# A planned instruction order: activation-table loads taken out of the plan and written in afterwards

## The chip, the cores and the metric

The kernel runs on one core of a Trainium2 chip. A core has four engines that compute: PE (TensorE, matrix products), DVE (VectorE), ACT (ScalarE, which applies functions such as exp from a loaded table and also copies), and POOL (GpSimd). SP (SyncE) issues most DMAs. Each engine runs its own instructions strictly in the order in which they stand in its queue, and waits for the others at semaphores. The metric is device time of one execution in microseconds (us).

## The reference, cut to what matters

The input is 8 sequences of 256 tokens with 128 channels in float32. Eight blocks follow each other; after each one stands `x = layernorm(x + block(x))`:

1. a gated linear recurrence (sigmoid gates, exp, running product and running sum along the sequence);
2. two layers of local attention (8 heads of 64, window 64, l2-normalised queries and keys), each with a GELU feed-forward of width 341;
3. a selective scan ("mamba": silu, softplus, and 16 states for each of 256 inner channels, stepped along the sequence);
4. a mixture of 32 experts, one for each token, capacity 80;
5. two attentions with 16 heads and a feed-forward each, over chunks of 32 tokens and across chunks;
6. a mixture of 8 experts, two for each token, capacity 320, and a shared expert of width 1024;
7. causal attention with 16 heads of 8, rotated and decaying by head;
8. a linear layer with ternary weights and a bias.

## The kernel before

The kernel has six stages (`STAGES`): `rglru` (block 1 for the first four sequences), `local_mamba` (block 1 for the other four, blocks 2 and 3), `moe1` (4), `chunked` (5), `moe2` (6) and `typed` (7 and 8). In `local_mamba` eight sequences pass through attention and then the scan as a software pipeline; four sequences are alive at a time. For each sequence the scan runs eight rounds (lines 1295 to 1300): ACT makes four decay factors `da` with exp, DVE forms a product `hs`, scans it, forms a second product, and PE sums the result into `y`. A round costs about 5 us of DVE.

Mixtures are routed on the chip. For `moe1`, `route1` computes a row number for each token, in two pieces: tiles 0 to 13 (the first seven sequences), then tiles 14 and 15 (line 1512 writes the numbers `put`, line 1523 the numbers `get`). `scatter` (line 1616) then issues one indirect DMA on POOL for each tile of 128 rows, which writes them to the table `places` in memory. Plain DMAs (`got<-places`, line 1636) bring the table back once all 16 are done, and the experts' matmuls start with the transposes `bt` (line 1643). For `moe2`, `route2` does the same with 32 indirect writes; the results come back by indirect gathers (line 1651) on POOL, most of them made to wait, one each, for a silu of the shared expert.

**Who sets the order.** The program text emits all instructions. Then `_Order` takes the list and reorders it. `plan` is a list scheduler: it walks through a model of the five queues, and whenever an engine is free it takes, of the instructions that are ready, the one with the lowest `rank`. A rank is the instruction's place by priority plus a hand-tuned offset from `BIAS` (engine, tile name, stage). How long an instruction occupies its engine, and when its result is out, comes from the table `LENGTHS` (nanoseconds, two numbers). `impose` then pins each engine's queue to the planned order. The times in the plan decide nothing but order.

**ACT's tables.** exp and ln come from one table set, silu, gelu and sigmoid from three others. A function whose set isn't loaded needs a load first (`ACT_TABLE_LOAD` in the trace, `LoadActFuncSet` in the program). The kernel asks for the exp-and-ln set itself, by `exp_ln`, which emits a load at a fixed place: after the sigmoids (line 1017), after the gelus (line 1194), after the silus (line 1245), and at a few more places; `keep` ties it to ACT's instruction just before. In `moe1` a load of the silu set stands behind the last routing exp (line 1528). For all other functions the compiler puts a load right in front of an instruction whose set is not the one it finds in place. In the planner a load is an instruction of its own: `group` puts it into group 1 with exp and ln, `change` charges nothing for it, and its length is 1178 or 1283 ns; a change of group among ACT's functions is charged with `TABLE` (1283 ns) as well. `STAY` is what a change of group costs in rank: 70 for PE (where the groups are array shapes) and 310 for ACT.

Lines in the text and in the profile are those of the kernel before. In the kernel after, the same statements stand up to 17 lines away.

Of the kernel before, what the change touches and what calls it, by code (L numbers as in the profile page):

```python
# [309 lines left out]
class _Order:  # L310
# [12 lines left out]
    STAY = dict(PE=70, ACT=310)  # L323
    BIAS = {
        "ACT  1": 495, "ACT  3": -495, "ACT d 2": -1445, "ACT e 4": -700, "ACT e 6": 370, "ACT fh 4": -30, "ACT four 4": 630, "ACT four 5": -345,
        "ACT ge 2": 385, "ACT got 3": 50, "ACT got 5": 590, "ACT k 2": -275, "ACT kp 4": -40, "ACT lakq 2": -75, "ACT lavp 2": -95, "ACT lg 2": 620,
        "ACT lnrs 1": 225, "ACT lnrs 2": -280, "ACT lnsq 2": 40, "ACT ot 6": 75, "ACT ptsb 2": -740, "ACT qsq 2": -5, "ACT r 2": -70, "ACT rg 1": -590,
        "ACT rg 2": -320, "ACT rn 2": 55, "ACT rs 4": -50, "ACT rs 6": -25, "ACT s 6": -190, "ACT savp 2": -5, "ACT sg 3": 560, "ACT sh 5": -250,
        "ACT spl 1": -410, "ACT spt 1": -15, "ACT st 6": 460, "ACT v 2": 25, "ACT xc 2": -2725, "ACT xchunked 2": -400, "ACT xchunked 4": -390,
        "ACT xs 2": 10, "ACT xsq 4": -660, "DVE ab 4": 720, "DVE bt 3": -1225, "DVE bt 5": 190, "DVE centre 0": -205, "DVE d 2": -10,  # L330
        "DVE decaypart 4": -240, "DVE e 2": 50, "DVE four 5": 105, "DVE fs 4": 10, "DVE gate 2": -345, "DVE gate 5": -320, "DVE get 2": 180, "DVE get 4": 5,
        "DVE get 5": 850, "DVE got 4": -40, "DVE h 2": 5, "DVE h 5": -525, "DVE hs 2": 5, "DVE k 5": -680, "DVE lares 2": -200, "DVE lg 4": 665,
        "DVE nm 2": -135, "DVE nm 6": -95, "DVE oh 2": -285, "DVE oh 4": 2440, "DVE oh 5": -180, "DVE ptsb 2": 20, "DVE ptsb 6": -250, "DVE put 2": 190,
        "DVE put 4": 480, "DVE q 5": 470, "DVE q 6": 785, "DVE r 2": -120, "DVE rc 2": -270, "DVE rc 4": 175, "DVE route 2": -345, "DVE s 2": 20,
        "DVE s 5": -95, "DVE s 6": 1585, "DVE sares 2": 30, "DVE sel 4": -50, "DVE sg 3": -250, "DVE sm 4": 365, "DVE spt 1": 810, "DVE st 6": 150,
        "DVE sum 2": -705, "DVE t 5": 400, "DVE th 4": 650, "DVE u 2": 255, "DVE vec 2": 50, "DVE we 4": -30, "DVE wlocal 2": 1325, "DVE xc 2": -1830,
        "DVE xla 4": -580, "DVE xlf 4": 75, "DVE xlocal 2": -860, "DVE xmoe 6": 10, "DVE xpf 4": -10, "DVE xrglru 2": 205, "DVE xsa 4": 485, "DVE ys 3": 100,
        "DVE z 4": -190, "PE a 2": 50, "PE acc 5": 10, "PE b 2": 30, "PE bt 3": 1010, "PE bt 5": -580, "PE cum 2": 80, "PE cum 4": -1270, "PE fold 2": 105,
        "PE g 2": -700, "PE gate 1": -345, "PE gate 2": 345, "PE hps 4": -15, "PE kps 4": 95, "PE lg 2": 205, "PE lin 6": -1140, "PE ln 1": 355,
        "PE ln 2": -45, "PE o 6": -910, "PE out 4": -35, "PE pg 5": -20, "PE proj 5": 100, "PE proj 6": -570, "PE ps 4": -455, "PE pt 2": -25,  # L340
        "PE pt 4": -125, "PE pu 3": 2550, "PE pu 5": -720, "PE py 3": 740, "PE qkt 2": -1425, "PE raw 2": -1360, "PE rows 2": 585, "PE sc 2": -60,
        "PE sc 4": 30, "PE sc 6": -1215, "PE v 5": 470, "PE v 6": -20, "PE vps 2": 1025, "PE vps 4": -10, "PE wo 2": 60, "PE wo 6": -855, "PE wout 2": -95,
        "PE xps 2": -790, "PE y 2": 20, "PE z 2": 40, "PE zt 4": -20, "POOL biasrows 3": -595, "POOL e 4": 415, "POOL e 6": -305, "POOL got 5": 490,
        "POOL km 5": 665, "POOL mean 0": 635, "POOL one 0": 395, "POOL places 2": -70, "POOL places 5": -240, "POOL q 5": 50, "POOL q 6": -325,
        "POOL rest 4": -990, "POOL rg 1": -25, "POOL rows 4": 85, "POOL ss 2": -20, "POOL t 2": 595, "POOL u 2": 110, "POOL zero 0": -35,
        "POOL zeros 1": -385, "SP bc 2": 200, "SP cst 3": -455, "SP got 3": 535, "SP got 5": 505, "SP outdram 6": 275, "SP places 1": 1460,
        "SP rottable 0": 45, "SP routetables 0": 495, "SP rows 4": -370, "SP scales 2": 40, "SP vec 0": -1475, "SP wattn 2": 15, "SP wmoe 2": -150,
        "SP wmoe 4": -150, "SP wmoe 5": -100, "SP xs 2": -660,
# [88 lines left out]
    def group(self, i):  # L437
        x, e, op = self.ops[i]
        if e == "PE":
            up = lambda v: 32 if v <= 32 else 64 if v <= 64 else P  # L440
            ap = x.ins[1].bass_ap.ap
            return up(ap[0][1]), up(int(np.prod([k for _, k in list(ap)[1:]])))
        if e == "ACT":
            return 1 if op == "LoadActFuncSet" else self.SETS.get(str(x.func).split(".")[-1]) if op == "Activation" else None
        return None
# [319 lines left out]
class _Kernel:  # L765
# [125 lines left out]
    def exp_ln(self, last=None):  # L891

        i = self.nc.scalar.preload_act_table_set("natural_log_exp_and_others")
        if last is not None:
            self.issue_after([i], last)
# [1504 lines left out]
```

## Time and profile before

| what | value |
|---|---|
| median of 3 runs | 1695.54 us (1694.59 to 1696.02) |
| the profiled execution, its own time | 1695.66 us |
| span of that execution in the trace | 1692.0 us |
| mean granted TensorE clock | 0.947 |
| busy: PE, DVE, ACT, POOL | 1442.4, 1138.2, 976.5, 579.2 us |
| share of the chain of waits: PE, DVE, ACT, "issue", POOL, DMA | 49, 23, 11, 9, 5, 2% |
| `rglru` and the start of attention, 0 to 60 us: busy PE, DVE, ACT | 25.1, 33.7, 32.0 us |
| `local_mamba`, about 60 to 800 us | PE busy 601.2, DVE 602.5, ACT 551.2 of 740 us |
| `moe1` with its routing, about 800 to 860 us | PE busy 33.1 of 60 us |
| `chunked`, about 860 to 1285 us | PE busy 409.9 of 425 us |
| `moe2`, about 1285 to 1455 us | PE busy 156.3 of 170 us |
| `typed`, about 1455 to 1692 us | PE busy 216.8 of 237 us |

The span is the time from the first to the last instruction on the core; the execution's own time is 3.66 us more. In the views, a row of a table by stretches gives the stretch, its length, then for PE, weight loads (PEld), DVE, ACT and POOL the busy time and the number of instructions, then the granted clock, the DMA share and GB/s. A row of a timeline gives start, duration, engine, line, operation and tiles as out<-in; in brackets stands how long the engine sat idle before and what ended that.

### The profile page before, as it was taken

How to read it: one execution, taken by the hardware profiler on the slowest of the kernel's cores; microseconds unless marked ns; L12 is line 12 of the kernel's file. 1: busy time of each engine (PE TensorE's matmuls, PEld its weight loads, DVE VectorE, ACT ScalarE, POOL GpSimd, SP SyncE). 2: the span in 40 equal slices, each digit the busy share in tenths (PEclk: the TensorE clock that was granted, in tenths of full speed). 3: DMA queues.
4: the chain of work that ended last, by engine and by line, in shares of the span. 5: the costliest groups of instructions: out<-in, count | busy, mean ns of one | idle time of the engine just before them, and what ended most of it. 6: DMA issues, size and time to landing. Idle time of an engine off the chain costs nothing.

```text
span 1692.0 us, 28693 instructions
## 1 busy us (share of the span) xinstructions
PE 1442.4 (85%) x10858; PEld 932.5 (55%) x10858; DVE 1138.2 (67%) x2182; ACT 976.5 (58%) x2661; POOL 579.2 (34%) x535
## 2 busy tenths in 40 slices
PE   2688897979788877676679999999997998999997
PEld 1355553545454544343557776766674764566664
DVE  5755579898989898689354656566445332588885
ACT  3777887787877868644135554545443222366654
POOL 1344462616263423100331222221214004567573
PEclk7799999999999998899789999999997998999998
DMA  5000012121212213266310000000102121000000
GB/s 193 1 1 1 1 39 63 39 63 39 63 39 63 64 38 97 66 196 242 111 47 2 8 14 11 7 8 5 46 2 68 47 82 30 18 5 4 8 4 10
DMA packets 45113, 77.97 MB, mean 46 GB/s; under 512 B 5580, under 2 KB 21988, under 8 KB 43824
## 3 DMA queue, kind: packets, MB, share of 16 engines
q1 hardware_dynamic: 39648, 70.02, 13.8%
q0 software_dynamic: 3216, 5.07, 1.1%
q8 instruction: 85, 1.39, 0.3%
q10 hardware_dynamic: 2112, 1.05, 0.2%
q14 instruction: 52, 0.43, 0.1%
HBM read 66.87 MB, written 10.76 MB: 46 GB/s over the span
## 4 chain that ended last, share of the span: by engine, by line
PE 49%; DVE 23%; ACT 11%; issue 9%; POOL 5%; DMA 2%; another core or an unknown queue 0%; SPq 0%; ACTq 0%; DVEq 0%; POOLq 0%
PE vps L863 7%; PE kps L863 6%; PE sc L863 5%; PE out L863 4%; DVE hs L1299 3%; DVE hs L1300 3%; PE pu L863 3%; PE pg L863 3%; PE pt L974 3%; DVE hs L1297 2%; PE o L863 2%; ACT e L1146 2%; PE hps L863 2%; PE py L863 2%; PE acc L863 2%
## 5 line engine op out<-in xcount | busy, mean ns | idle before, releaser
L863 PE MATMUL y<-hs,ident 128*128 128x512 f32 x256 | 136.7, 647 | 30.2 <-DVE hs L1300 29.9
L1151 POOL TENSOR_TENSOR e<-e,rc 128x1024 f32<-128x1024 f32 x32 | 79.6, 2486 | 228.3 <-DVE rc L1150 227.6
L1299 DVE TENSOR_TENSOR_SCAN hs<-da,hs 128x1024 f32<-128x1024 f32 x64 | 154.1, 2409 | 0.1
L2250 ACT ACTIVATE e<-sc,nm 128x128 f32<-128x128 f32 (+1 forms) x256 | 105.1, 426 | 64.1 <-DVE nm L2245 55.2
L974 PE MATMUL pt<-ident,e 128*128 128x128 f32 x768 | 119.2, 281 | 18.0 <-POOL e L1151 12.4
L1295 ACT ACTIVATE da<-d,na 128x255 f32<-128x255 f32 x256 | 110.5, 508 | 22.5 <-DVE hs L1299 20.2
L1146 ACT ACTIVATE e<-sc,nm,rn 128x128 f32<-128x128 f32 x256 | 114.7, 468 | 10.9 <-DVE nm L1141 10.5
L974 PEld LDWEIGHTS pt<-ident,e 128*128 128x128 f32 x768 | 88.4, 143 | 56.3 <-issue 19.2
L2253 POOL TENSOR_TENSOR e<-e,rc 128x1024 f32<-128x1024 f32 x48 | 91.1, 1897 | 65.6 <-DVE rc L2252 65.5
L1829 POOL TENSOR_TENSOR e<-e,rc 128x512 f32<-128x512 f32 x32 | 33.9, 1059 | 226.1 <-DVE rc L1828 173.4
L1098 POOL TENSOR_TENSOR t<-t,t 128x512 f32<-128x512 f32 x64 | 84.1, 1316 | 61.1 <-DVE t L1085 56.0
L1651 POOL DMA_INDIRECT got<-ybuf,get x48 | 45.7, 952 | 169.0 <-DMA ybuf<-ys 87.6
L1804 ACT COPY kp<-kps 128x512 f32<-128x512 f32 x128 | 74.8, 585 | 48.5 <-PE kps L863 46.7
L1297 DVE TENSOR_TENSOR hs<-u,bc 128x1024 f32<-128x1024 f32 x64 | 87.5, 1384 | 6.2 <-POOL u L1284 5.5
L863 PEld LDWEIGHTS y<-hs,ident 128*128 128x128 f32 x256 | 47.5, 204 | 77.9 <-DVE hs L1300 47.5
L1300 DVE TENSOR_TENSOR hs<-hs,bc 128x1024 f32<-128x1024 f32 x64 | 87.5, 1369 | 0.0
L863 PE MATMUL qk<-w_local,h 128*128 128x512 f32 x128 | 71.1, 644 | 13.0 <-DVE t L1085 6.2
L976 DVE COPY ptsb<-pt 128x512 f32<-128x512 f32 x104 | 69.0, 677 | 17.0 <-PE pt L974 16.0
L1840 ACT COPY vs<-vps 128x512 f32<-128x512 f32 x64 | 37.4, 584 | 67.5 <-PE vps L863 56.8
L863 PE MATMUL vps<-sa_vp,x_lf 128*32 128x512 f32 x512 | 69.8, 594 | 0.0
L976 ACT COPY ptsb<-pt 128x512 f32<-128x512 f32 x88 | 51.4, 584 | 31.3 <-PE pt L974 30.7
L2245 DVE TENSOR_REDUCE nm<-sc 128x4 f32<-128x1024 f32 (+1 forms) x48 | 58.3, 1215 | 15.2 <-PE sc L863 14.6
(380 smaller groups left out, 3800.0 us busy)
## 6 DMA issues: line engine op xcount, KB each, us to landing
bc<-xs SPq DMA_DIRECT2D x128, 256.0 KB
w_moe<-in_e_dram SPq DMA_DIRECT2D x16, 768.0 KB
w_attn<-in_w_dram SPq DMA_DIRECT2D x4, 1024.0 KB
w_local<-in_w_dram SPq DMA_DIRECT2D x2, 1557.0 KB
places<-zeros SPq DMA_DIRECT2D x2, 1280.0 KB
got<-places SPq DMA_DIRECT2D x6, 256.0 KB
ybuf<-ys SPq DMA_DIRECT2D x8, 160.0 KB
x_in<-in_x_dram SPq DMA_DIRECT2D x1, 1024.0 KB
```

Source lines behind the costliest of these rows:

```text
L863: return self.nc.tensor.matmul(out, lhsT, rhs, start=start, stop=stop)
L974: self.last = self.nc.tensor.transpose(pt[:, j * P : (j + 1) * P], src[:, j * P : (j + 1) * P], self.ident)
L976: copy(sb.rearrange("p a b -> p (a b)"), pt)
L1098: nc.gpsimd.tensor_add(t1, t1, t2)
L1146: nc.scalar.activation(e[:, j, g, :], scs[:, j, g, :], AF.Exp, bias=nm[:, j, g : g + 1], scale=rq[:, j, g : g + 1], accum_out=sm[:, j, g : ...
L1151: nc.gpsimd.tensor_tensor(e, e, rc.unsqueeze(3).to_broadcast([P, 2, 4, P]), ALU.mult)
L1295: nc.scalar.activation(da[:, n, c, 1:S], d[:, c, 1:S], AF.Exp, scale=na[:, i : i + 1])
L1297: nc.vector.tensor_tensor(hs, u.unsqueeze(1).to_broadcast(shp), bn, ALU.mult)
L1299: nc.vector.tensor_tensor_scan(line(hs), line(da), line(hs), 0.0, ALU.mult, ALU.add)
L1300: nc.vector.tensor_tensor(hs, hs, cn, ALU.mult)
L2250: nc.scalar.activation(e[:, i, :], sc[:, i, :], AF.Exp, bias=nm[:, i : i + 1], accum_out=sm[:, i : i + 1])
L2253: nc.gpsimd.tensor_tensor(e, e, rc.unsqueeze(2).to_broadcast([P, n, keys]), ALU.mult)
```

## The change

Six things are changed.

- The planner no longer sees loads of a table. All calls of `exp_ln`, the load of the silu set on line 1528, and `exp_ln` and `keep` themselves are gone, with the ties that they made.
- After planning, `impose` walks through ACT's planned queue and writes one load of the exp-and-ln set in front of each exp or ln that follows a function of another group (and in front of the first).
- `STAY` becomes 120 for PE and 190 for ACT.
- `BIAS` has 174 entries for 183, of which nearly all values differ.
- `LENGTHS` is taken anew. Most entries move by a few ns. The three indirect or POOL-issued forms become 1280 ns of POOL each: writes to `places` from 995, gathers from 949, `msk` from 741.
- The tie of one exp in `typed_weights` (line 2164) to a load goes.

```diff
-    STAY = dict(PE=70, ACT=310)
+    STAY = dict(PE=120, ACT=190)
     BIAS = {
...
     LENGTHS = {
-        "ACT  LoadActFuncSet  ": (1178, 1283), ...
-        "POOL got DMACopy 128x128 2560x128": (949, 2493),
-        "POOL places DMACopy 2560x128 128x128": (995, 2277),
+        "POOL got DMACopy 128x128 2560x128": (1280, 2500),
+        "POOL places DMACopy 2560x128 128x128": (1280, 2500),
...
         if e == "ACT":
-            return 1 if op == "LoadActFuncSet" else self.SETS.get(str(x.func).split(".")[-1]) if op == "Activation" else None
+            return self.SETS.get(str(x.func).split(".")[-1]) if op == "Activation" else None
...
         if e == "ACT":
-            return 0.0 if op == "LoadActFuncSet" else self.TABLE
+            return self.TABLE
...
     def impose(self):
         order, _ = self.plan()
+        ring, last = [], None
+        for i in order["ACT"]:
+            g = self.groups[i]
+            if g is not None:
+                if g == 1 != last:
+                    load = self.tc.nc.scalar.preload_act_table_set("natural_log_exp_and_others")
+                    self.ops.append((load.ins, "ACT", "LoadActFuncSet"))
+                    ring.append(len(self.ops) - 1)
+                last = g
+            ring.append(i)
+        order["ACT"] = ring
         for ring in order.values():
...
-    def keep(self, i):
...
-    def exp_ln(self, last=None):
-
-        i = self.nc.scalar.preload_act_table_set("natural_log_exp_and_others")
-        if last is not None:
-            self.issue_after([i], last)
-        self.keep(i)
-        return i
...
-        self.exp_ln(last)
...
-            self.exp_ln(nc.scalar.activation(xc, xc, AF.Silu))
+            nc.scalar.activation(xc, xc, AF.Silu)
...
-        i = nc.scalar.activation(lg, lg, AF.Exp)
-        if t0:
-
-            j = nc.scalar.preload_act_table_set("silu_and_others")
-            self.issue_after([j], i)
-            self.keep(j)
+        nc.scalar.activation(lg, lg, AF.Exp)
...
-            self.exp_ln_load = self.exp_ln()
...
-                if b == 0:
-                    self.exp_ln(self.silu)
...
-            self.exp_ln(self.silu)
...
-        self.issue_after([i], self.exp_ln_load)
```

## Prediction

> **What bounds the kernel now.** First comes the chain of waits, for which engine sets the end, with the page's groups beside it.
>
> ```profile
> PE 49%; DVE 23%; ACT 11%; issue 9%; POOL 5%; DMA 2%; another core or an unknown queue 0%; SPq 0%; ACTq 0%; DVEq 0%; POOLq 0%
> ...
> L1299 DVE TENSOR_TENSOR_SCAN hs<-da,hs 128x1024 f32<-128x1024 f32 x64 | 154.1, 2409 | 0.1
> ...
> L1295 ACT ACTIVATE da<-d,na 128x255 f32<-128x255 f32 x256 | 110.5, 508 | 22.5 <-DVE hs L1299 20.2
> ```
>
> ACT has 11% of the chain, so most of its work is hidden. The two groups show how: the 64 scans on DVE waited 0.1 us in all, though their input `da` comes from ACT, while `da` itself waited 20.2 us for scans. In the scan rounds ACT runs ahead of DVE, and a load saved between two `da` is worth nothing there.
>
> Second, busy time by stretch, for the places that the change touches.
>
> ```profile
> 45.50:67.00 21.50, 14.80 (x45) 6.28 (x46) 14.52 (x35) 19.93 (x26) 6.45 (x6) 0.79 0.00 1
> ...
> 67.00:76.00 9.00, 7.61 (x30) 3.79 (x29) 8.24 (x4) 4.51 (x8) 2.61 (x2) 0.74 0.01 2
> ...
> 255.00:340.00 85.00, 71.49 (x420) 41.30 (x420) 77.64 (x92) 67.09 (x176) 37.92 (x35) 0.98 0.20 51
> ...
> 797.00:821.50 24.50, 8.49 (x25) 3.87 (x23) 11.40 (x37) 3.67 (x7) 16.57 (x17) 0.68 0.29 110
> 821.50:825.00 3.50, 0.00 (x0) 0.00 (x0) 0.29 (x1) 0.00 (x0) 0.78 (x2) 0.50 0.65 187
> ```
>
> The fourth engine column is ACT: 19.93 of 21.50 us in the first row, so ACT bounds this stretch alone, and none other. From 67 to 76 us DVE does (8.24 of 9.00). In the scan rounds DVE does (77.64 of 85). In the routing of `moe1` POOL is the busiest (16.57 of 24.50) and PE works a third of the time, then not at all for 3.5 us. Beyond that PE bounds: 409.9 of 425 us in `chunked`, 216.8 of 237 us in `typed`.
>
> Third, ACT's timeline in the first stretch.
>
> ```profile
> 51.41 1.28 ACT L1091 ACT_TABLE_LOAD   x1
> 52.71 0.22 ACT L1091 ACTIVATE rn<-ss 128x16 f32<-128x16 f32 x1
> ...
> 53.92 1.28 ACT L1092 ACT_TABLE_LOAD   x1
> 55.21 0.21 ACT L1092 ACTIVATE rn<-rn 128x16 f32<-128x16 f32 x1
> 55.44 1.28 ACT L1013 ACT_TABLE_LOAD   x1
> ...
> 61.28 1.28 ACT L1017 ACT_TABLE_LOAD   x1
> ...
> 63.73 1.28 ACT L893 ACT_TABLE_LOAD   x1
> ```
>
> Eight loads stand between 45.50 and 66 us, 10.3 us of the 21.5: sigmoid gates (1013) and the ln and exp of the l2 norm (1091, 1092) alternate. The one at 63.73 is written by `exp_ln` right behind the return at 61.28, and changes nothing that the next exp needs: a doubled return.
>
> **What moves.** I compared the built orders of both kernels. All instructions are the same but for the loads: 74 before, 64 after, at 1283 ns each, 12.8 us less on ACT. Thirteen fall to 8 up to 66 us; from there to 800 us 55 fall to 50 (seven doubled returns go, two before line 1146 and five before 1295; one more excursion to silu adds a pair); the last six stay. The cost of leaving the loads out of the plan would be a load that used to run while ACT waited and now stands at the last moment. There was little such cover: ACT idled 4.9 us in all inside the excursions of the local stages. The load of line 1528 ran at 814.25 while ACT idled, and now stands before the first silu of the experts; that silu waits until 828.90 for PE's `pg`, and the load has 2.15 us of slack behind ACT's copy. I cost it at nothing; uncovered it would cost 1.28.
>
> **1. The start, -7 us.** From 45.50 to the second copy of `k` at 74.24, ACT's new queue holds 15.1 us of work with four loads, so ACT alone could reach that copy's end (74.83 before) at 60.6: 14.2 us sooner. The steps between on POOL (t, 1.3 us each), DVE and PE's transposes keep it from that; following them through I get about 64 to 65 for the copy, and 8 to 10 us for the first row maximum `nm` (line 1140, at 75.33). But DVE was not idle there: from 63.75 to 74.6 it had 10.9 us of the second `rglru` group, one reciprocal of 6.54 among it, and this must now find other room. The bounds are 0 (DVE, 8.24 of 9.00 busy, takes it all back) and 14.2. I take the middle, 7.
>
> Here the Trainium skill ("ScalarE: Activation LUTs", section "What ACT_TABLE_LOAD costs") would make the change worth more: it gives a drain of about 1380 ns beside each load's 1283, so that ten loads would be an estimated 26.6 us instead of 12.8. The rows above show no drain: the load at 51.41 and the function behind it at 52.71 are 1.30 us apart. By the rows the smaller figure holds.
>
> **2. The scans, 76 to 797 us, -2 us.** Five loads fewer are 6.4 us of ACT at most; -9 if all seven doubled ones stood on the path. Five of the seven stand before `da`, which runs ahead of the scans (0.1 us of waiting), so those are worth nothing; the two before line 1146 are worth up to 1.28 each, since `e` stands on the chain (2%). The added pair costs 0 to 2.6. The order of DVE hardly moves: the work that stands ahead of the k-th scan differs by 3 us or less, with either sign. From 108 to 255 us PE (130.0 of 147) and ACT (121.1) share the bound, so ACT's order counts there. I take -2, from the two loads; the bounds are -9 and +13 (2.6, 3, and a silu pair and a doubled wait of the new order, 1.3 to 2.6 on each of three sequences).
>
> **3. The writes of `moe1`, -2.7 us.**
>
> ```profile
> 796.25 2.28 DVE L1299 TENSOR_TENSOR_SCAN hs<-da,hs 128x1024 f32<-128x1024 f32 x1
> 798.45 0.14 DVE L1512 CAST put<-route 128x14 int32<-128x14 f32 x1
> ...
> 799.48 1.32 POOL L1616 DMA_INDIRECT places<-x_chunked,put  x1 [50.34 <-DVE get L1523]
> 801.11 0.99 POOL L1616 DMA_INDIRECT places<-x_chunked,put  x1 [0.30 <-issue]
> 802.40 0.97 POOL L1616 DMA_INDIRECT places<-x_chunked,put  x1 [0.30 <-issue]
> ```
>
> Sixteen writes follow each other every 1.28 us (0.97 busy, 0.30 idle), to 820.21, and only then can `got` and the transposes `bt` (825.04) start. The old plan counted 995 ns for one. With 1280 the planner sees the row longer and puts `put` one scan sooner, behind the scan at 791.80: 4.4 us. So 14 writes end at about 795 + 14 x 1.28 = 812.9. The last two need `put` of the last tiles (813.43 before), ahead of which four small route steps on DVE (0.61, 0.62, 0.24, 0.17, with ACT's 0.58 between) now stand before the last product, up to 1.6 us later: 815, then two writes, 817.5. That is 2.7 sooner than 820.21. Bounds: -4.4 (the whole scan) and +1.6 (the last two set it alone). For the 32 writes of `moe2` PE has the shared expert beside them; I cost these at nothing, and at 8 x 0.3 = 2.4 us if that cover is gone.
>
> **4. From `moe2` to `typed`, -2 us.** In POOL's new queue two products `km` (line 2205, at 1457.91 and 1464.72, 1.9 us each), which PE's first scores wait for, stand ahead of the last gathers instead of between them. SP's queue holds the same transfers and is not passed. PE idles 2.93 us in 1455 to 1470 and 0.74 in 1470 to 1490: bounds -3.7 and 0. I take about half.
>
> **5. `chunked` and `typed`, 0 us.** PE is 96% and 91% busy with the same matmuls; STAY 120 keeps array shapes together more. In `typed` the transposes `pt` come one matmul group sooner. In before POOL's product `e` (1.90) ended a median of 2.5 us before its `pt`, and 0.53 in the closest of six units; `pt` 1.09 sooner could wait 0.56 in each of 8: +4.7. `o` waited 2.3 us for `pt`'s copies: -2.3. `chunked` can move by 1.5 either way.
>
> **The sum.** 7 + 2 + 2.7 + 2 + 0 = 13.7 us. The profiled execution's own time is 1695.66 (span 1692.0 and 3.66 around it), 0.12 above the median of the runs, which is nothing. 1695.66 - 13.7 = **1682.0 us**. A gain under 0.2%, 3.4 us, is about what a measurement of this kernel can't tell from no change.
>
> **Rivals.**
>
> - *The start gives all it has*: 14.2 there, and up to 9 in the scans, with 2.7 + 2 from parts 3 and 4: 27.9, 1667.8. For it: ACT is 93% busy in the first stretch and the doubled loads stand on its chain. Against it: DVE's 8.24 of 9.00 behind, and the 0.1 us of line 1299.
> - *The gain is given back*: DVE's 10.9 us moves into the stretch behind, where PE and ACT are 88% and 82% busy, and only part 3 is left: 1693, no change. For it: the chain has only 11% of ACT.
> - *Slower, by one mechanism*: the planner, which no longer counts the loads' own rank and place, lets ACT fall behind, and DVE, in order, waits in front of its scans for `da`. A sequence pays when ACT's lead over the scan is spent; at 2 us a sequence, over seven sequences, the 14 us of gain are gone, at 3 us it is 21: 1695.66 - 13.7 + 21 = 1703. Against it: one pair more, 2.6 us, is all that the built order adds, and 0.1 us of wait says that the lead is there now.
> - *The loads don't go*: excluded by the built order, which has ten fewer.
>
> **How the numbers follow.** The forecast's case (some 4 to 22 us faster) has 0.60, the full start 0.14, given back 0.10, slower 0.16. The range 1664 to 1698 takes in the first three and the mild end of the fourth; half of the fourth and a little of the second lie outside. Faster 0.60 + 0.14 = 0.74, within 0.2% 0.10, slower 0.16.
>
> **What would show it.** Loads 64, ACT's busy time some 12.8 us less. Part 1: second `k` at about 65 and the first `nm` 5 to 10 us sooner; the first scan of `local_mamba` sooner by about 7. Part 2: line 1299 still without idle; if it waits for line 1295, the fourth case holds. Part 3: the last indirect write near 817.5 less whatever was gained ahead of it, `bt` 4.8 us behind it. Part 4: PE's idle in the first 35 us of `typed` down from 3.7. Part 5: `pt` waiting for POOL's `e` on line 2253. Wrong it is if the time between the first `nm` and the last scan grows by more than the start gained.

## The result, and the profile after

| what | before | after |
|---|---|---|
| median of 20 runs | 1695.71 us (1693.65 to 1698.13) | 1701.78 us (1694.07 to 1705.22) |
| ratio, 95% interval | 1 | 1.0026 (1.0018 to 1.0034) |
| span of the profiled execution | 1692.0 us | 1701.4 us |
| mean granted TensorE clock | 0.947 | 0.931 |

The change makes the kernel slower, by 0.26% (the ratio is near that of the means; the two medians alone would give 1.0036). The forecast was 1682.0, and the range ended at 1698. Four of the 20 runs of the kernel after (1694.1 to 1695.6 us) are as quick as before, and the profiled one, 1703.59 us, is among the slower ones, so the views show more loss (9.4 us) than the medians do (6.1). These are the page's lines of the kernel after: busy time, the chain of waits, the scans.

```profile
PE 1448.9 (85%) x10858; PEld 936.1 (55%) x10858; DVE 1145.6 (67%) x2182; ACT 963.4 (57%) x2651; POOL 575.5 (34%) x535
...
PE 51%; DVE 21%; ACT 13%; issue 7%; POOL 5%; DMA 2%; another core or an unknown queue 1%; SPq 0%; ACTq 0%; DVEq 0%; POOLq 0%
...
L1293 DVE TENSOR_TENSOR_SCAN hs<-da,hs 128x1024 f32<-128x1024 f32 x64 | 153.1, 2398 | 0.1
```

ACT is busy 13.1 us less (976.5 before), as worked out, and yet ACT's share of the chain rises from 11 to 13%. The scans still wait for nothing. To see where the time is, the span is cut at events that both kernels have:

| stretch | before | after | difference | forecast |
|---|---|---|---|---|
| start to the first row maximum `nm` | 75.3 | 64.0 | -11.4 | -5 to -10 |
| first `nm` to the first scan of `local_mamba` | 179.3 | 194.1 | +14.8 | 0 |
| first scan to the last | 541.6 | 545.9 | +4.3 | -2 |
| last scan to the first `bt` | 28.8 | 27.1 | -1.7 | -2.7 |
| first `bt` to the last product of `moe1` | 25.9 | 30.8 | +4.9 | 0 |
| from there to `chunked` | 11.2 | 11.1 | -0.1 | 0 |
| `chunked` | 426.4 | 415.0 | -11.4 | 0 |
| `moe2` | 173.4 | 176.3 | +2.9 | 0 |
| `typed` | 230.1 | 237.1 | +7.0 | -2 |

The rows sum to +9.4 us. Two large gains, one forecast and one not, are outweighed by five losses; the first gain and the first loss belong together, as the timelines below show. The first two stretches of the prediction's second view, and the scans, in the kernel after:

```profile
45.50:67.00 21.50, 17.06 (x80) 9.71 (x79) 16.05 (x36) 16.83 (x27) 8.10 (x8) 0.92 0.01 2
67.00:76.00 9.00, 3.58 (x36) 1.79 (x34) 7.71 (x4) 5.34 (x18) 0.00 (x0) 0.69 0.00 0
...
258.10:804.00 545.90, 443.77 (x2369) 253.39 (x2370) 480.68 (x556) 391.44 (x994) 176.90 (x151) 0.93 0.28 79
```

ACT (fourth engine column) no longer fills the first row. From 67 us DVE is 7.71 of 9.00 us busy with four instructions, the work of the second `rglru` group, while PE (first column) does 3.58. This work has not moved. DVE's longest piece of it, first in before, then in after, and POOL's first product `e` in after:

```profile
68.02 6.54 DVE L1028 RECIPROCAL rg<-rg 128x1024 f32<-128x1024 f32 x1
```

```profile
67.56 6.54 DVE L1023 RECIPROCAL rg<-rg 128x1024 f32<-128x1024 f32 x1
```

```profile
76.80 2.77 POOL L1146 TENSOR_TENSOR e<-e,rc 128x1024 f32<-128x1024 f32 x1 [18.01 <-DVE rc L1145]
```

In after the first `nm` gets ahead of the reciprocal, but `rc`, which the same softmax needs from DVE next, stands behind it and behind the second `nm` (76.53 us, where ACT's exps for it end at 72.3), and POOL has been idle for 18.01 us when it comes. The last product of the second `rglru` group starts at 86.33 us in before and at 86.12 in after, the third row maximum at 106.0 and 106.6: by then nothing is left of the 11.4 us. The next view, DVE's waits from 250 to 800 us, is where part 2 was to be read; first before, then after (total, times, longest).

```profile
DVE t L1277 <- ACT e L1275: 18.6, 6, 5.5
DVE x_mamba L918 <- ACT ln_rs L917: 7.4, 5, 3.7
DVE s L1312 <- PE wout L863: 6.8, 3, 3.8
...
DVE x L1179 <- PE wo L863: 3.0, 3, 1.0
```

```profile
DVE s L1306 <- PE wout L873: 11.2, 3, 6.2
DVE x L1174 <- PE wo L873: 7.7, 3, 4.5
...
DVE t L1271 <- ACT e L1269: 7.0, 5, 3.7
```

No wait for `da` appears. DVE waits less for ACT's exps directly and more for PE's products `wout` and `wo`: the waits have moved, not gone.

### The profile page after: what moved, and what is told of

Read it like the earlier page. It is cut to its first block, busy times and chain, and to the rows that moved or that the text cites. A ratio compares the mean times of both kernels' runs of the same rounds, so it can differ in the third digit from the quotient of the medians.

```text
span 1701.4 us, 28696 instructions
## 1 busy us (share of the span) xinstructions
PE 1448.9 (85%) x10858; PEld 936.1 (55%) x10858; DVE 1145.6 (67%) x2182; ACT 963.4 (57%) x2651; POOL 575.5 (34%) x535
## 3 DMA queue, kind: packets, MB, share of 16 engines
q1 hardware_dynamic: 39648, 70.02, 13.7%
## 4 chain that ended last, share of the span: by engine, by line
PE 51%; DVE 21%; ACT 13%; issue 7%; POOL 5%; DMA 2%; another core or an unknown queue 1%; SPq 0%; ACTq 0%; DVEq 0%; POOLq 0%
PE vps L873 7%; PE kps L873 7%; PE sc L873 6%; PE out L873 4%; ACT e L1141 4%; PE pt L970 3%; PE pg L873 3%; PE pu L873 3%; DVE hs L1293 3%; PE o L873 3%; DVE hs L1294 2%; DVE hs L1291 2%; PE qk L873 2%; PE py L873 2%; PE hps L873 2%
## 5 line engine op out<-in xcount | busy, mean ns | idle before, releaser
L873 PE MATMUL y<-hs,ident 128*128 128x512 f32 x256 | 142.9, 673 | 31.1 <-DVE hs L1294 30.9
L873 PE MATMUL qk<-w_local,h 128*128 128x512 f32 x128 | 70.5, 642 | 13.1 <-DVE t L1080 4.8
L873 PE MATMUL vps<-sa_vp,x_lf 128*32 128x512 f32 x512 | 66.3, 594 | 0.6 <-ACT vs L1827 0.6
L2037 DVE TENSOR_TENSOR sh<-sh,pu 128x512 f32<-128x512 f32 x32 | 22.0, 687 | 64.1 <-PE pu L873 51.5
```

Of the source, the lines that this page charges most:

```text
L873: return self.nc.tensor.matmul(out, lhsT, rhs, start=start, stop=stop)
```

## The experiments

Two explanations of the loss ahead of `moe1` were to be told apart. **A**: the new tables (`BIAS`, `STAY`, `LENGTHS`) give a worse order there. **B**: the loads, which the plan no longer holds, stand in worse places. Later **E** made B sharper: a load written at the last moment is exposed, and one written straight behind the last function of another set would not be. Besides, each late stage was given the other kernel's order by itself. Ratios are to the kernel before on the same chip, with 95% intervals; `last scan` is the start of the 64th. For one stage alone, the planner reads the other kernel's tables in that stage only, and the order of all other stages stays as it was:

```diff
+    MIX = {4}                      # chunked; {0, 1, 2}, {5, 6} in others
...
-        ... x.bass_priority + self.BIAS.get(f"{k} {g}", 0) ...
+        ... x.bass_priority + (self.BIAS2 if g in self.MIX else self.BIAS).get(f"{k} {g}", 0) ...
```

and the same for `LENGTHS` and `STAY`.

**e1: the loads alone.** The kernel after, with the three tables of before.

> The changed planner and loads (64), with the old STAY, BIAS and LENGTHS. Theory A, the new tables cost the time and the loads cost none: the order of chunked, moe2 and typed is that of before, the last scan ends no later than before (796.25 start, 0 to 8 us sooner) and the time is 1686 to 1694 us; only the silu load of moe1 costs 1.3 us more. Rival B, ACT falls behind because the plan no longer sees the loads: the last scan is 4 to 8 us late as in the changed kernel and the time is 1698 to 1704 us.

Measured: 1.0115 (1.0095 to 1.0136); last scan 824.9, 28.7 us later than in before. A would have had no loss here; B stands, though the loss is far above the 4 to 8 us at the last scan that it named (the whole time is 19 us more by the ratio). DVE's waits from 250 to 800 us in e1:

```profile
DVE t L1270 <- ACT e L1268: 20.4, 6, 6.6
DVE ss L1073 <- ACT qsq L1072: 10.7, 11, 2.8
...
DVE x L1204 <- PE w L872: 7.1, 3, 6.5
```

They are waits for ACT, and for PE behind ACT. Much of it is the order, not the places of the loads: without loads in it, the plan with the old tables also puts other work between the two silus of a sequence (64 loads, where the order of before needs 62), and e6 below, which has the order of before and the same late loads, is only 11.6 us late. The first `nm` comes at 75.6 us, as in before, although 8 loads stand up to 66 us as in after: fewer loads alone don't bring it forward.

**e14: the tables alone.** Before, with the new tables in `rglru`, `local_mamba` and their joint stage (`MIX = {0, 1, 2}`), its loads planned as ever.

> The kernel before, its loads planned (89 of them come out), with the new tables for the stages up to the scans. The fourth cell of old and new tables against planned and unplanned loads; last scan so far 797.0 (old, planned), 825 (old, unplanned), 802.6 (new, unplanned). If the new tables bring the sooner nm and its loss by themselves: first nm about 64 us, first scan 256 to 259. If the loss behind nm is the unplanned loads': nm about 64, first scan 250 or sooner. With 25 loads more on ACT the last scan is 805 to 820.

Measured: 1.0203 (1.0185 to 1.0221). `nm` comes at 67.6 (64.0 in after), the first scan at 260.1, the last at 836.9. So the tables alone are worse still; part of that is that this order needs 89 loads, 15 more than before. The four kernels make a square of the last scan: old tables and planned loads 797.0 (mean of three profiles), old and unplanned 824.9, new and unplanned 803 (mean of six), new and planned 836.9. A and B each hold by itself and neither is the whole: tables and the plan's view of the loads belong together, each half of the change costs 28 and 40 us at the last scan without the other (19 and 34 us of the whole time), and together they come back to 6 us behind where they began. e14 also shows that the early `nm` is no gain with planned loads either: its third row maximum comes at 106.7 us.

**e6: before's order, the loads written late.** All engines keep the order of before; the loads that `exp_ln` asks for are planned but taken out afterwards, and the rule of the change writes them. 62 loads, 12 fewer than before.

```diff
+        for i in order["ACT"]:
+            if any(self.ops[i][0] is x for x in self.tc.planned):
...
+                continue
...
+                if g == 1 != last:
+                    load = ...preload_act_table_set("natural_log_exp_and_others")
```

> The kernel before in its own order on every engine, unchanged, with the exp-and-ln loads written afterwards by the rule of the change: 62 loads for 74, 15.4 us less of ACT, nothing else. Theory A, the loads on the path are few and what they give at the start is given back: 0 to 5 us faster (ratio 0.997 to 1.000), the first nm 3 to 6 us sooner, the first scan 0 to 2 us sooner. Rival, the loads bound the start and the scans as the forecast had it: 7 to 13 us faster (0.992 to 0.996).

Measured: 1.0042 (1.0028 to 1.0056); last scan 807.8, 11.6 later. Fewer loads and a slower kernel, with nothing else changed but their places.

**e10: the same, each load where before had it.** The 12 doubled loads are dropped; the other 62 stand at the places they had.

```diff
+            if any(self.ops[i][0] is x for x in self.tc.planned):
...
+                if last != 1:
+                    load = ...preload_act_table_set("natural_log_exp_and_others")
...
+                    last = 1
+                continue
...
```

> The kernel before in its own order, with the 12 doubled loads left out and the other 62 at the places that they have before. With the run that kept the order and wrote the loads late (ratio 1.0042, last scan 11.6 us late) this tells leaving out from late placing. Theory E: ratio 0.996 to 0.9995, first nm 2 us sooner, last scan 0 to 5 us sooner. Rival F: removing loads shifts ACT against the other engines and costs as before: ratio 1.002 to 1.005.

Measured: 0.9986 (0.9965 to 1.0008). Twelve loads less, 15 us of ACT, are worth between a small loss and 6 us, at the middle 2. e6 and e10 have the same instructions in the same order but for the places of the loads: this alone is 1.0042 against 0.9986. The two ran on different chips, but the profiles put the difference where no chip differs: the last scan comes at 807.8 us in e6 and 803.5 in e7 (the same order and places up to there), at 799.9, 794.4 and 797.5 in e10, e11 and e18, and at 797.5 in e8, which has the order of before on the chip of e6. On the mean the late places cost 8.4 us there, and the 12 loads fewer are worth nothing that these profiles show. ACT's timeline at one return from silu shows how. In before:

```profile
747.44 0.63 ACT L1245 ACTIVATE xc<-xc 128x512 f32<-128x512 f32 x1 [1.91 <-DVE xc L1235]
...
748.56 1.28 ACT L893 ACT_TABLE_LOAD   x1
...
750.91 0.37 ACT L1252 COPY xs<-xps 33x256 f32<-33x256 f32 x1 [0.46 <-PE xps L863]
752.17 0.56 ACT L1273 ACTIVATE e<-raw,vec 128x256 f32<-128x256 f32 x1 [0.89 <-PE raw L863]
...
753.98 0.64 ACT L1275 ACTIVATE e<-e 128x512 f32<-128x512 f32 x1
```

In e6:

```profile
756.07 0.63 ACT L1262 ACTIVATE xc<-xc 128x512 f32<-128x512 f32 x1 [1.91 <-DVE xc L1252]
...
759.57 0.36 ACT L1269 COPY xs<-xps 33x256 f32<-33x256 f32 x1 [1.90 <-PE xps L880]
761.87 0.56 ACT L1290 ACTIVATE e<-raw,vec 128x256 f32<-128x256 f32 x1 [1.94 <-PE raw L880]
...
763.82 1.28 ACT L765 ACT_TABLE_LOAD   x1
765.11 0.63 ACT L1292 ACTIVATE e<-e 128x512 f32<-128x512 f32 x1
```

The silu `xc` is the last function before the return; the next that needs the other set is the exp `e<-e`. Between them stand copies that wait for PE. Before loads ahead of them, and ACT then sits idle 0.46 and 0.89 us; e6 idles 1.90 and 1.94 at the same copies and loads after, with `e<-e` waiting: 6.5 us from silu to exp become 9.0. The kernel after does the same:

```profile
751.76 0.63 ACT L1239 ACTIVATE xc<-xc 128x512 f32<-128x512 f32 x1 [0.56 <-DVE xc L1229]
754.26 0.36 ACT L1246 COPY xs<-xps 33x256 f32<-33x256 f32 x1 [1.87 <-PE xps L873]
756.27 0.56 ACT L1267 ACTIVATE e<-raw,vec 128x256 f32<-128x256 f32 x1 [1.64 <-PE raw L873]
...
758.22 1.28 ACT L759 ACT_TABLE_LOAD   x1
759.51 0.63 ACT L1269 ACTIVATE e<-e 128x512 f32<-128x512 f32 x1
```

Over the returns to exp from 60 to 800 us, ACT's idle time between the last function of another set and the load is 0.4 us in before, 13.8 in e6 and 8.9 in after. That idle time could have held the loads. From the start of that function to the exp or ln behind the load, 24 returns take 81.2 us in e6 and 71.4 in e11, which has the places of before.

**e9 and e12: the loads straight behind the last function** (E), and in e12 with `moe1`'s silu load early as well.

```diff
-        ring, last = [], None
+        ring, last, at = [], None, -1
...
-                    ring.append(len(self.ops) - 1)
-                last = g
+                    ring.insert(at + 1, len(self.ops) - 1)
+                last, at = g, len(ring)
```

> The changed kernel with its order kept on every engine; only the place of the exp-and-ln loads differs: each stands straight behind the last silu, gelu or sigmoid instead of in front of the next exp or ln (45 instructions stood between in the scan stage). Theory E, the late place costs the time because a load that comes early runs while ACT would wait for the copies' inputs, and one that comes late has nothing to hide behind: 4 to 9 us faster than the changed kernel, ratio 0.997 to 1.001, the last scan 3 to 7 us sooner. Rival F, the order of the new tables loses it, and the place is nothing (the idle time around the loads was 9 us, of which a load could use 5.8 at most): within 2 us of the changed kernel, ratio 1.003 to 1.005.

> The changed kernel with the exp-and-ln loads early and the silu load of moe1 early too. Theory E: 1 to 4 us less than with the exp-and-ln loads alone early, since the first experts then start 1.3 us sooner and leave PE's half clock sooner. Rival: no more than 0.5 us.

Measured: e9 1.0059 (1.0038 to 1.008), last scan 809.0; e12 1.0048 (1.0035 to 1.006), last scan 806.3. Six profiles of the order and places of after have it at 801.0 to 804.0. E as stated falls: loads written early are no better than loads written late. A reason lies near, though no run tests it by itself: at 12 of the 26 returns of after the instructions between the function and the load don't wait, and an early load pushes them back. It was left to say which of the two places is right for each load.

**e13: only into idle time.** A load goes to the first gap of over 0.5 us that the plan has on ACT between the last function and the exp, and otherwise stays. Four of 64 move (at about 117, 565, 700 and 759 us).

```diff
-                    ring.append(len(self.ops) - 1)
-                last = g
+                    idle = [m for m in range(at + 1, len(ring)) if self.start[ring[m]] - self.start[ring[m - 1]] - self.cost(ring[m - 1])[0] > 500] if at >= 0 else []
+                    ring.insert(idle[0] if idle else len(ring), len(self.ops) - 1)
+                last, at = g, len(ring)
```

**e15** is the kernel after, unchanged, on the same chip.

> The changed kernel with four of its 64 loads moved, all else in its order: the returns at 117, 565, 700 and 759 us go from in front of the exp or ln to the first place behind the silu where the plan has ACT idle for over 0.5 us (ahead of a copy that waits for PE). Theory E, refined (a load costs its 1.28 us where it stands behind a wait, and nothing where it stands in it): 2.5 to 5 us faster than the changed kernel on the same chip, the last scan 2.5 to 4 us sooner. Rival F, places are worth nothing: within 1 us.

> The changed kernel, unedited, beside the others on one chip: ratio 1.002 to 1.005.

Measured: e13 1.0021 (1.0002 to 1.004), 1676.36 us; e15 1.0038 (1.0024 to 1.0053), 1681.08 us. The medians are 4.7 us apart and the ratios 2.8, and the two intervals overlap. In the profiles the exp or ln behind each moved load comes 0.7 to 1.4 us sooner after the function ahead of it, 4.6 us in all; the last scan comes 1.5 sooner, at 801.9, which lies within the 801.0 to 804.0 of the unmoved loads. So the places of these four loads shorten the returns, and what that is worth in the whole time, between nothing and some 5 us, is not settled.

**e4: the silu load of `moe1` early.**

```diff
+                if g == 2 and last == 1 and self.stage[i] == 3:
+                    load = ...preload_act_table_set("silu_and_others")
...
+                    ring.insert(at + 1, len(self.ops) - 1)
...
```

> The changed kernel with the silu load of moe1 put back behind the last exp of the routing, where ACT idles; nothing else moves. Theory A: the first silu of the experts starts 1.3 us sooner after bt (5.6 us behind it for 6.85), and the time is 1.3 us less if that is all, up to 5 us less if PE's clock also comes up sooner: 1697 to 1700.5 us. Rival: the first product waits for PE's pg and pu anyway: no change, 1701.8 us.

Measured: 1.0019 (1.001 to 1.0028); `bt` to the last product 27.8 us against 30.8 in after. But e15, without this edit, has 27.8 too, so those 3 us are not the load. e12 against e9 has 34.2 become 27.8, and medians 3.5 us apart with overlapping intervals. What the late load costs is not settled between 0 and some 3 us.

**e2 and e7: `chunked` alone in the new order**, on before (`MIX = {4}`) and on e6.

> The kernel before, with the new tables (STAY, BIAS, LENGTHS) for the chunked stage alone; the other stages keep their order. Theory A: the stage is 11 us shorter, as in the changed kernel (lag +10.9 us at its start, -0.5 at its end), PE busy 8 us less in it, the time 1683 to 1687 us. Rival C, the 11 us come back in chunked only because work left over from moe1 is hidden there when it starts late: the stage is as long as before, 1694 to 1697 us.

> The same with the new tables for the chunked stage: the candidate for the best version. The sum of the two parts: 0.9987 times that of the kernel with its order kept, 0.996 to 0.999 by theory A, 0.991 to 0.995 by the rival.

Measured: e2 0.9987 (0.9977 to 0.9997), `chunked` 411.0 us; e7 0.998 (0.9966 to 0.9994), `chunked` 415.3 against 423.7 in e6. The 11.4 us of the table are not the same everywhere. e2's chip runs the kernel before in 1676.25 us, 19 less than the chip of the first result, and there `chunked` takes 412.0 us in e1, which has before's order in that stage. The same 1024 matmuls in the same order, first in before, then in e1 on the other chip (busy, mean ns, idle ahead of them):

```profile
L863 PE MATMUL out<-vs,ptsb 128*32 128x128 f32 x1024 | 48.0, 275 | 4.8 <-issue 4.7
```

```profile
L872 PE MATMUL out<-vs,ptsb 128*32 128x128 f32 x1024 | 42.6, 274 | 0.0
```

"issue" says that PE stood still and waited for nothing that the profile shows. Laid side by side, the two runs part in nine or ten jumps of 0.8 to 1.9 us, 14 us in all, most of them in these matmuls, and nearly all within 5 us of a transfer on a queue of instructions. That nearness says nothing: these transfers come some 11 us apart, so four fifths of all moments of the stage lie as near to one. Instruction fetches are a guess here, not shown. In the new order the row has 1.1 us of "issue" (40.3 us busy) on the first chip. So the gain in `chunked` is mostly one of these stalls where they are seen (423.3 to 426.4 us with the old order, 415.0 to 416.0 with the new), and 1 to 3.5 us elsewhere (412.0 to 412.9 and 409.4 to 410.9). Why some chips show them stays open.

**e3 and e8: `typed` and `moe2`'s end alone**: after with the old tables there, and before with the new (`MIX = {5, 6}`).

> The changed kernel with the old tables for moe2 and typed. Theory A: the 9.9 us lost between 1288 us and the end are in the order of these two stages; the time is 1690 to 1694 us. Rival D, the loss follows from when the gathers start or from the clock, whatever the order: 1699 to 1703 us.

> The kernel before with the new tables for moe2 and typed alone. If the order of these stages is what loses 5 to 10 us at the end of the changed kernel: moe2 2 us shorter, typed 5 to 7 us longer, ratio 1.002 to 1.004. If the loss comes from the state in which typed begins (clock, gathers), whatever the order: ratio 0.999 to 1.001.

Measured: e3 1.005 (1.0031 to 1.0068), `typed` 231.8 us against 235.7 in e4 on the same chip; e8 1.0012 (0.9991 to 1.0033), `typed` 236.9 against 230.4 in e6 on the same chip. All profiles agree that the new order makes the stage longer, by 4 to 6.5 us between runs on the same chip: it takes 230.1 to 231.8 us in the eleven with the old order and 235.7 to 237.1 in the nine with the new. The times don't follow as clearly: e8's interval holds 1, and e3, which should be quicker than after, isn't. PE's waits in `typed`, in after and then in before:

```profile
PE zt L950 <- DVE s L944: 8.5, 7, 2.3
PE pt L970 <- DVE ptsb L972: 3.8, 4, 2.6
PE o L873 <- DVE ptsb L972: 2.9, 13, 0.3
PE proj L873 <- DVE x_moe L951: 2.1, 1, 2.1
```

```profile
PE zt L954 <- DVE s L948: 8.0, 13, 2.3
PE o L863 <- DVE ptsb L976: 2.3, 7, 0.6
...
PE pt L974 <- POOL e L2253: 0.2, 1, 0.2
```

The transposes `pt` now wait 3.8 us, not for POOL's `e` but for DVE's copy `ptsb`, which frees their buffer.

**e16: the gathers of `moe2` later**: none behind the steps of the shared expert's second quarter, two instead of one in those of the third.

> The changed kernel with the gathers of moe2's results spread: none are issued through the second quarter of the shared expert, two in each step of the third. On chips where PE stood still for 9 to 11 us at 1410 us this came 10 us into 13 to 15 gathers in a row, and ended 2.5 us behind the last. If the row of gathers holds PE up, the stop shrinks to under 3 us and the kernel is 5 to 8 us faster there; if PE's instruction fetch alone does it, it stays; on a chip without the stop nothing is to be seen.

Measured: 1.0044 (1.0029 to 1.0059), `moe2` 162.6 us, as short as in e15 (164.2). It was meant for a standstill that the first chip shows near 1410 us in both kernels (in after, DVE's copy at 1420.17 waits 8.76 us); this chip has none, so the run tells nothing of it. Other profiles tell a part: e1, e2, e10 and e18, on chips without the standstill, also have 15 gathers in a row, and PE has no pause of over 1.2 us beside them. So the row of gathers alone does not stop PE.

**e5: the kernel after again**, on a chip that shows the stalls, beside e6 to e8.

> The changed kernel once more, unedited, so that it has a profile and times beside the experiments of this call. On the chip of the first four experiments PE's stalls of 1 to 9 us behind instruction fetches (14 us in the chunked stage of before, 5 us in that of the changed kernel, 9 and 11 us at 1410 us) are absent from the traces. If the loss is the order's, the ratio is 1.002 to 1.004 with or without them; if it is the longer stall at 1412 us (2.5 us more) and the run's chip, it is 0.998 to 1.001 where the stalls are absent.

Measured: 1.0049 (1.003 to 1.0068), 1704.49 us against 1695.8. The stalls are there, so e5 by itself does not part its two cases; e15, where they are absent, does. In the first result, e5 and e15 after is 1.0026, 1.0049 and 1.0038 of before: the loss is there with the stalls and without.

**e11, e18 and e17: a version that beats both.** e11 is e10 (before's order and places, the 12 doubled loads dropped) with the new `chunked`. e18 is e11 again, and e17 is e11 with one offset changed, so that `put` and with it the indirect writes start earlier:

```diff
-        "DVE put 2": 190,
+        "DVE put 2": -300,
```

> The same with the new tables for the chunked stage alone: the candidate for the best version. Theory E: the sum of both, ratio 0.990 to 0.997 (the chunked part was worth 2.7 us on a chip without PE's stalls and about 11 on one with them). Rival F: 0.998 to 1.001.

> The best version so far, unedited, beside it on the same chip: ratio 0.997 to 0.999.

> The best version so far (order of before, doubled loads left out, new tables for chunked) with the rank offset of DVE's put lowered from 190 to -300, so that the row numbers of the first 14 tiles are written some scans sooner; DVE's order changes in 16 places around the last scans and nothing else moves. Part 3 of the forecast by itself: the 14 writes are done before the last two tiles' row numbers, which then set the end: from the last scan to bt 25.5 to 27 us for 28.8, 1.5 to 3.5 us faster than the best version on the same chip (ratio 0.996). Rival: four small route steps and put ahead of the last scans push these back by as much: within 0.7 us.

Measured: e11 0.9979 (0.9969 to 0.9988), e18 0.998 (0.997 to 0.999), e17 0.9968 (0.9956 to 0.998): 1670.08 us, where before takes 1675.2. POOL's timeline of e17:

```profile
778.94 1.32 POOL L1732 DMA_INDIRECT places<-x_chunked,put  x1 [32.46 <-DVE route L1638]
...
802.34 0.97 POOL L1732 DMA_INDIRECT places<-x_chunked,put  x1 [0.31 <-issue]
815.32 0.97 POOL L1732 DMA_INDIRECT places<-x_chunked,put  x1 [12.01 <-ACT lg L1641]
816.59 0.97 POOL L1732 DMA_INDIRECT places<-x_chunked,put  x1 [0.30 <-issue]
```

and of e18:

```profile
800.73 1.32 POOL L1732 DMA_INDIRECT places<-x_chunked,put  x1 [50.34 <-DVE get L1639]
...
820.50 0.97 POOL L1732 DMA_INDIRECT places<-x_chunked,put  x1 [0.30 <-issue]
```

The first write is 21.8 us sooner and the last 3.9, of which 2.4 is the last scan's. The last two writes, which wait for the routing of the last tiles, now set the end by themselves (12.01 us of idle before them), so there is no more to be had from the first fourteen. e17 and e18 overlap in their intervals; both lie below 1.

## Why the prediction was wrong

From the forecast of -13.7 to the +9.4 us of the profiles it is 23.1 us: 10.4 up to the first scan, 6.3 in the scans, 1.0 in the writes, 4.9 in `moe1` and 11.9 in `moe2` and `typed`, less 11.4 in `chunked`. No one step carries it.

**The step that failed for the loads** is "There was little such cover: ACT idled 4.9 us in all inside the excursions". Idle time was the wrong measure of cover. Where a load already stands in a wait, the wait is filled by the load, and no idle time is left to see; in before there were 22 instructions between the functions and their loads over all returns and 0.4 us of idle ahead of the loads, because the loads had been planned into the waits. The cover is what ACT would idle if the load were not there, and e6 shows it: 13.8 us, and a last scan some 8 us later. From this misreading came the cost of nothing for late loads and the size of what ten fewer loads are worth (e10, with twelve fewer: some 2 us). That it also gives part 2 its sign is argued for the kernel after, whose order is another: there e13 settles nothing and e9 found the early place no better.

**Part 1, the start (-7).** The near end came: `nm` 11.4 us sooner, a little beyond the 5 to 10 named. The far end did not, the first scan came 3.5 later. The step that failed is "this must now find other room", with the middle of two bounds taken for it: DVE's 10.9 us of the second `rglru` group did not move (its reciprocal at 67.56 us for 68.02), the first `nm` only got ahead of them, and by the third row maximum the gain was gone. So the bound of 0, DVE takes it all back, was the answer for the start; the 3.5 us beyond it go with the tables, for the first scan comes at 254.6 in e1 and at 260.1 in e14. The rival "the gain is given back", with 0.10, has the outcome; that DVE's work moves into the stretch behind is not how it came. What moved `nm` was the order that the tables make more than the loads: e1, with the old tables and the eight loads, has it at 75.6 us, e14, with the new tables and planned loads, at 67.6.

The drain that the Trainium skill ("ScalarE: Activation LUTs", section "What ACT_TABLE_LOAD costs") puts beside each load is not in the kernel after either: the load at 758.22 takes 1.28 us, and `e<-e` starts at 759.51, 0.01 behind it. By its larger figure the loads left out would have been worth more, by the runs they were worth hardly anything.

**Part 2, the scans (-2).** It was +4.3, inside the bounds of -9 and +13. The rival for "slower" had the right origin, a planner that no longer counts the loads, and the wrong place: `da` at the scans, still 0.1 us. The waits stand where the returns are, at `e`, `xs` and the products behind them, before a sequence's scans begin. The lead of `da` over the scans says nothing about these.

**Part 3, the writes (-2.7).** Right in size: -1.7 in after, -3.0 and -3.1 in e5 and e15, -1.6 in e17 against e18. `put` now runs ahead of the last scan, but not for the reason given, which makes this partly luck: the writes' 1280 ns, set by itself in `LENGTHS` of before, gives the very program that before is; what moved `put` is the other entries of the tables (in e1, with the old ones, the first write comes behind the last scan, in e14 ahead of it). The kernel after's timelines of DVE and POOL:

```profile
800.62 0.15 DVE L1505 CAST put<-route 128x14 int32<-128x14 f32 x1
```

```profile
801.65 2.92 POOL L1604 DMA_INDIRECT places<-x_chunked,put  x1 [50.00 <-DVE put L1505]
804.87 2.22 POOL L1604 DMA_INDIRECT places<-x_chunked,put  x1 [0.30 <-issue]
...
824.04 0.97 POOL L1604 DMA_INDIRECT places<-x_chunked,put  x1 [1.23 <-issue]
```

The last scan starts at 804.0. The first two writes take 5.1 us instead of 2.3, while DVE still works on the scans, and eat the missing part.

**`moe1` (0).** "The load has 2.15 us of slack" was the step that failed, and it was wrong in kind. ACT's timeline in after, and PE by stretches in after and in before:

```profile
836.69 1.28 ACT L1688 ACT_TABLE_LOAD   x1 [3.84 <-PE pg L873]
837.99 0.44 ACT L1688 ACTIVATE sg<-pg 128x320 f32<-128x320 f32 x1
```

```profile
831.10:845.40 14.30, 13.67 (x63) 13.08 (x64) 2.27 (x4) 4.08 (x7) 0.00 (x0) 0.50 0.19 46
845.40:861.90 16.50, 16.50 (x151) 16.34 (x150) 7.10 (x13) 3.83 (x8) 0.00 (x0) 1.00 0.58 194
```

```profile
825.00:829.50 4.50, 4.46 (x21) 4.27 (x22) 0.69 (x1) 1.02 (x2) 0.00 (x0) 0.50 0.60 146
829.50:850.90 21.40, 21.40 (x194) 21.24 (x192) 9.40 (x16) 5.66 (x11) 0.00 (x0) 1.00 0.52 158
```

The load that the compiler puts ahead of a silu starts only when the silu's own input `pg` is there: ACT idled 3.84 us and then the load took its 1.28 in the open. The larger part of the 4.9 us is another: PE's granted clock stays at 0.50 for 14.3 us of this stretch, in before for 4.5. In e5 and e15, the kernel after again, it does so for 6.6 and 6.7 us and the stretch takes 27.8 us, 3 less, so this is partly the one execution.

**Part 4 and `typed` (-2 and 0).** The step that failed is the 0 for `typed`, taken between bounds of -2.3 and +4.7: the stage is 7.0 us longer, and 4 to 6.5 in e3 and e8, each against a run on its own chip. The bound of +4.7 (8 times 0.56 are 4.5) had the right size for `pt` waiting, 3.8, and the wrong releaser (DVE's copy, in place of POOL's `e`); the rest of the 7.0 is not laid at one wait. The first score product with `km` comes 2.3 us later than in before, though the shared expert's first matmul is 0.5 sooner. That is PE's standstill near 1410 us, 8.85 us here and 1.9 and 3.6 in before, which no term counted: on chips without it `moe2` takes 162.5 to 164.2 us with the new order and 164.4 to 166.3 with the old, so the -2 of part 4 was about right there.

**`chunked` (0, "can move by 1.5 either way").** Near on the chips without stalls (1 to 3.5), wrong on the one that was asked about (11.4). The profile of before did have the row that says so, 4.7 us of "issue" in front of `out`, but not the rest of it, which lies inside the busy time.

The time, 1701.78, lies near the slower rival's 1703, but by other terms than that rival's.

## What to carry to other kernels

To see what a planned wait-filler is worth, look at what stands behind it and what that waits for, not at idle time around it: a good plan leaves none to see. Moving the table loads to the latest place, without touching anything else, made a kernel with 12 fewer of them 0.4% slower (e6); dropping the doubled ones and leaving the rest in place lost nothing (e10); the earliest place, in the order of after, was no better than the latest (e9). And a step that comes sooner is a gain only if the next one that needs the same engine does too: the first `nm` came 11.4 us sooner and the third not at all. Offsets that were tuned under one model of the queues did badly under the other: the loads alone cost 1.2%, the tables alone, ahead of `moe1`, 2.0%, and the whole change 0.3%, so test such halves as a square before one of them is blamed.

## What the runs showed of the hardware

- The kernel before takes 1695 to 1696 us in two of five series of runs (the first, and chip 13) and 1675 to 1676 on three other chips. 14 us are PE's jumps in `chunked`; another 7 are in `moe2` (173.4 us, 166.1 in e2), where PE stands still near 1410 us, from 11 to 13 us into a row of 13 to 15 gathers that POOL issues without pause until 3 us after the last. What stops PE there stays open; the same row passes without a stop on the other chips.
- A load of a set that is already there costs the full time: the doubled loads of before took 1.28 us each, like all others.
- At the start of `moe1`, after a pause of PE, the granted clock is 0.50 and comes back after 4.5 us of matmuls in before and after 14.3 in after (rows above). In e5 and e15, the same program as after, it comes back after 6.6 and 6.7, with the same pause of 0.59 us between PE's first groups; what decides is not shown.
- The indirect writes take 0.97 us each while DVE rests, and 1.4 to 2.9 for many of those that run while DVE works on the scans (in after the first two, in e17 seven of the first eleven).
